# Reordering the stages of a two-layer graph and expert kernel: pairs' transposes, first residual, router and preparation

## The chip, the cores and the metric
The kernel runs on one core of a Trainium2 chip. Its engines are PE (TensorE: matrix products and transposes, PEld being its weight loads), DVE (VectorE), ACT (ScalarE) and POOL (GpSimd); SP issues most of the DMAs. Each engine takes its instructions strictly in the order in which the program lists them for it, and waits on semaphores for the others. The metric is the device time of one execution, in microseconds. Before the change it is 1788.81, the median of six runs (1777.96 to 1794.82).

## The reference
64 batches of 256 rows with 256 columns go through two layers. Each layer is a graph attention with a residual, then a feed-forward part with a residual; every part starts with a layer norm.

```
x = x + elu(gat0(norm(x), adj))          # 4 heads of 64, one shared 256 x 256 mask
x = x + norm(x) @ Wf.T + bf
x = x + relu(gat1(norm(x), adj))         # 1 head of 256
t = norm(x)
x = x + t + sum over e of combine[e] * (gelu(t @ w1[e]) @ w2[e])   # best 2 of 8 experts
```
The attention of a layer is softmax over neighbours of leaky_relu(e_src + e_dst), times the projected rows. All arithmetic is fp32. The expert part includes its own tokens, so its result is the normed rows plus the weighted expert outputs.

## The kernel before
**Stages of a batch.** A batch is 256 rows, held as two tiles of 128 partitions. `batch_layers` (from line 384) is a generator; each `yield` ends a segment. The outer loop (from line 913) counts steps and runs one segment of every active generator in each step. A new batch starts every third step, so 6 batches are under way at a time and one *period* of three steps issues one whole batch's worth of work. The number that a `yield` gives is the rank of the generator's next segment: within a step the segments run in rising rank, and among equal ranks the one that started first. So the program's order, which is each engine's order, is written out by the ranks. The segments, with the phase of the step (its number modulo 3) and the rank:

| segment | phase, rank | work |
|---|---|---|
| 0 | 0, 40 | load of the batch three ahead, norm of x (DVE), transposes `pt` (PE), copy to `xT` (ACT) |
| 1 | 1, 20 | first projection `pq` (L329, 268 columns), exponentials (L337 ACT), scaling of q (L341 DVE) |
| 2, 3 | 2, 10 and 0, 10 | scores of heads 0-1, then 2-3: `pd` (L353 PE), `z` (L360 DVE, four each) |
| 4 | 1, 50 | values `pv` (L374, 65 columns), `rinv` (L381 DVE), `hp` (L402 DVE) |
| 5 | 2, 20 | elu and residual: exponential (L408 ACT), x1 and x1b (L411, L412, L414 DVE) |
| 6 | 0, 30 | norm and transposes of x1 |
| 7 | 1, 70 | feed-forward `pf` (L422), x2 (L428 DVE), its norm |
| 8 | 2, 60 | transposes of x2 |
| 9 | 0, 20 | second projection `pq` (259 columns), exponentials, scaling |
| 10 | 1, 10 | second scores: two `pd`, two `z` |
| 11 | 2, 40 | second values `pv` (257 columns), `rinv` |
| 12 | 0, 5 | relu (L445 ACT) |
| 13 | 1, 60 | x2 plus relu, norm |
| 14, 15 | 2, 15 and 0, 50 | bias and scale; normed rows `xe` and `base` (L463, L468 ACT) |
| 16 | 1, 35 | `base` to the output (SP), transposes of `xe` |
| 17 | 2, 50 | router product `pl` (L489), logits `lg` (L493); with a chunk's last batch also `top_two` (L509) |

The reciprocal square roots of the norms are taken on POOL (L308, L309), for two batches at once.

**Routing and experts.** Batches are grouped into chunks: twelve of 4, six of 2, two of 1; two more batches are computed densely. After a chunk's last router product, `route` ranks the rows, sends each row to the regions of its two experts in DRAM (POOL, L755), and queues `expert_pair` jobs of 256 rows. A pair starts in phase 2. Its segments: load of its rows `xr` (rank 90), load of the expert's weights `we` (phase 0, 90), transposes `px` with the copy `sT` on ACT and the columns `to` and `w` on DVE (phase 1, 40), hidden product `ph` and gelu (phase 2, 30), second product `py` and bias to `y` (phase 0, 80), scaling of y on ACT (phase 1, 2). A scatter-add (POOL, L695) adds the rows to the output, each waiting for earlier ones. One to three pairs start in a period, eight in four periods in the middle of the run. Until the first chunk is routed there are none.

**Buffers.** All products go to eight PSUM banks, named `bank`, handed out as they come free. `hp` has two buffers.

**Preparation.** Ahead of the loop the masks are transposed, each attention's weights get the columns that give e_src and e_dst and are centred (`gnn_weights`, L139: DVE products and sums, `center` on PE and DVE), then the feed-forward and the router weights are transposed. This part has no written order: the compiler sorts it, together with the first steps of the loop, by what is ready. The load of batch 0 is the first on SP's queue. Experts' weights are loaded and packed by eight generators, one started in each step from step 4 (`SETUP_AT`).

Of the kernel before, what the change touches and what calls it, by code (L numbers as in the profile page):

```python
# [26 lines left out]
def kernel(  # L27
# [17 lines left out]
    nc = tc.nc  # L45
    B, N, D = x.shape
    E = router.shape[0]
    H = 4
# [44 lines left out]
    def load_batch(b):  # L93
        t = io.tile([P, NT, D], F32, tag="xin", name=f"xin_{b}", bufs=6)
        nc.sync.dma_start(
            out=t, in_=x_rows[b * N : (b + 1) * N, :].rearrange("(t p) d -> p t d", p=P)
        )
        return t

    AHEAD = 3  # L100
    xin = {0: load_batch(0)}


    ident = const.tile([P, P], F32, tag="ident", name="ident")
# [8 lines left out]
    adj_i = work.tile([P, NT, N], adj.dtype, tag="z", name="adj_i", bufs=6)  # L113
    nc.scalar.dma_start(out=adj_i, in_=adj.rearrange("(t p) j -> p t j", p=P))

    masks = []
    for layer, op in enumerate((ALU.is_gt, ALU.not_equal)):
        mf = work.tile([P, NT, N], F32, tag="xT", name=f"maskf{layer}", bufs=4)
        nc.vector.tensor_scalar(mf, adj_i, 0.0, None, op0=op)
        pm = bank("pm", [NT, N])  # L120
        for t in range(NT):
            for j in range(NT):
                nc.tensor.transpose(
                    pm[:, j, t * P : (t + 1) * P], mf[:, t, j * P : (j + 1) * P], ident
                )
        m = const.tile([P, NT, N], F32, tag=f"mask{layer}", name=f"mask{layer}")
        nc.vector.tensor_copy(m, pm)
        masks.append(m)

    def center(w, cols):  # L130

# [7 lines left out]
    def gnn_weights(w, a, heads, slope, name):  # L139

        d = D // heads
        wx = const.tile([P, KT, heads, d + 3], F32, tag=name, name=name)
        for k in range(KT):
            nc.sync.dma_start(
                out=wx[:, k, :, :d],  # L150
                in_=w[k * P : (k + 1) * P, :].rearrange("p (h d) -> p h d", h=heads),
            )
        av = work.tile([P, 2, d], F32, tag="e", name=name + "_a", bufs=1)
        nc.scalar.dma_start(out=av.rearrange("p s d -> p (s d)"), in_=rows_to_all(a, 2 * d))
        prod = work.tile([P, heads, d], F32, tag="hp", name=name + "_p")
# [14 lines left out]
        flat = wx.rearrange("p k h c -> p k (h c)")  # L170
        center(flat, heads * (d + 3))
        return flat

    wx0 = gnn_weights(w0, a0, H, SLOPE0, "wx0")
    wx1 = gnn_weights(w1g, a1g, 1, SLOPE1, "wx1")
# [5 lines left out]
    pw = bank("pw", [KT, D])  # L181
    for t in range(KT):
        for k in range(KT):
            nc.tensor.transpose(
                pw[:, k, t * P : (t + 1) * P], wf_in[:, t, k * P : (k + 1) * P], ident
            )
    nc.vector.tensor_copy(wfT, pw)
    center(wfT, D)
# [3 lines left out]
    nc.vector.tensor_scalar(bias_f, bias_f, -1.0, None, op0=ALU.add)  # L192
# [4 lines left out]
    pr = bank("pr", [KT, E])  # L197
    for k in range(KT):
        nc.tensor.transpose(pr[:, k, :], r_in[:, k * P : (k + 1) * P], ident[:E, :E])
    nc.vector.tensor_copy(rT, pr)  # L200

# [41 lines left out]
    def fill_spare():  # L243
# [7 lines left out]
        based.append(d.ins)  # L251
        yield 90


    setup = [lambda e=e: pack_expert(e) for e in range(E)] + [fill_spare]


    tri = const.tile([P, P], F32, tag="tri", name="tri")
# [125 lines left out]
    def batch_layers(b, c0, xng, lg):  # L384
# [12 lines left out]
        scores(q, H, range(2, 4), masks[0], probs)  # L397
        yield 50
        pvs, rinv = attended(q, H, probs)
        hp = work.tile([P, NT, D], F32, tag="hp", name="hp")  # L400
        for t, pv in enumerate(pvs):
            nc.vector.tensor_tensor(  # L402
                hp[:, t, :].rearrange("p (h d) -> p h d", h=H), pv[:, :, :HD],
                rinv[:, t, :, None].to_broadcast([P, H, HD]), ALU.mult,
            )
        yield 20
        ex = work.tile([P, NT, D], F32, tag="e", name="e", bufs=1)
        nc.scalar.activation(ex, hp, AF.Exp)  # L408

# [24 lines left out]
        xT = transposed(x2)  # L434
        yield 20
        q = projected(xT, wx1, 1, rstd)
        yield 10
        probs = []
        scores(q, 1, range(1), masks[1], probs)
        yield 40  # L440
# [41 lines left out]
            based.append(d.ins)  # L482
            nc.sync.nop()
        xT = transposed(xe[:, :, :D], *(("xTd", DENSE) if dense else ()))
        yield 50
        pl = bank("pl", [NT, E])
        for t in range(NT):
            for k in range(KT):
# [109 lines left out]
    def expert_pair(j, n, ids, ef, regs, needs):  # L598

        i = j % GROUP  # L600
        upto = min(j + GROUP, n)
        if i == 0:
            _, regs["e"] = nc.values_load_multi_w_load_instructions(
                ids[0:1, 0, j:upto], engines=[mybir.EngineType.SP], min_val=0, max_val=E - 1,
                skip_runtime_bounds_check_because=WHY,
            )
            _, regs["t"] = nc.values_load_multi_w_load_instructions(
                ids[0:1, 1, j:upto], engines=[mybir.EngineType.SP], min_val=0, max_val=E * CAP,
                skip_runtime_bounds_check_because=WHY,
            )  # L610
# [12 lines left out]
        we = io.tile([P, WROW], F32, tag="we", name="we", bufs=WBUFS)  # L623
        nc.sync.dma_start(
            out=we, in_=wpack[bass.ds(e_sp, 1), :, :].rearrange("e p c -> (e p) c")
        )
        yield 40
        px = bank("px", [KT, PAIR])
        for t in range(2):
            for k in range(KT):  # L630
                nc.tensor.transpose(  # L631
                    px[:, k, t * P : (t + 1) * P], xr[:, t, k * P : (k + 1) * P], ident
                )
# [132 lines left out]
    def later(rank):  # L766

        yield rank
        while (len(order_steps) - 1) % TICKS == 0:
            yield rank  # L770

    def route(c, row0, nt, n, last, xng, lg):
# [135 lines left out]

    batches = jobs()
    step, more, credit = 0, True, 0.0  # L910
    SETUP_AT = 4
    with tc.manual_schedule():
        while more or active or waiting or dense_jobs or scatters:
            phase = step % TICKS
# [63 lines left out]
```

## Time and profile before
| | us |
|---|---|
| median of six runs | 1788.81 |
| profiled execution, its own time | 1774.68 |
| its span, first to last instruction | 1773.0 |
| PE busy | 1578.4 |
| DVE busy | 1294.2 |
| ACT busy | 834.8 |
| POOL busy | 839.4 |

Busy time counts instructions that run on the engine. An idle time in brackets stands before the instruction that ended it, with what released it: `[0.64 <-ACT xT L319]` says that the engine stood for 0.64 us until ScalarE's copy to xT had ended. A PE group `x8` has eight matmul records, since a product in fp32 leaves two; a transpose leaves one. The mean granted PE clock is 0.962 of full speed. Times are from the span's start. The page's own limits hold: ends of matmuls are modelled, and a wait for several things is put down to the last.

The run falls into a head (to about 25 us, up to the first projection), a filling without expert pairs (to about 278, where the first pair is transposed), a middle, and a tail after the last batch (from about 1450), where pairs and dense experts remain.

### The profile page before, as it was taken

To read this page: it belongs to the slowest core of one execution; us is meant where nothing else is said; L and a number is where in the kernel's file an instruction comes from. 1 tells how busy PE (TensorE), PEld (TensorE's weight loads), DVE (VectorE), ACT (ScalarE), POOL (GpSimd) and SP (SyncE) were. 2 spreads that over 40 slices of the span, in tenths; PEclk is the share of its full clock that TensorE was granted. 3 is DMA by queue.
4 is the path that set the end of the run, shared out by engine and by line. 5 is a ranking of instruction groups with operands and counts; after the bars stand their busy time and mean duration, and the time that the engine had idled before them with its cause. 6 is when DMAs were issued, how large, how long until landed. Compare 5 with 4: busy or idle time off the path is not lost. (4 is left out here: it accounts for less than half of the span.)

```text
span 1773.0 us, 29975 instructions
## 1 busy us (share of the span) xinstructions
PE 1578.4 (89%) x9254; PEld 1389.3 (78%) x9254; DVE 1294.2 (73%) x4808; ACT 834.8 (47%) x1773; POOL 839.4 (47%) x788
## 2 busy tenths in 40 slices
PE   5898889799999999999999999999989998698791
PEld 4787777688888888888888888888878887577681
DVE  6888888978787878878787878789788886522231
ACT  1233324355555555555554555555455554533340
POOL 1111333426455564646464646565564655634444
PEclk9999999999999999999999999999999999888896
DMA  3510112135445453545453445445354455674753
GB/s 105 168 37 24 61 42 71 54 106 114 130 110 136 105 135 81 125 109 129 113 126 89 100 123 114 130 111 136 83 132 110 113 118 136 166 189 96 172 109 42
DMA packets 137372, 192.89 MB, mean 109 GB/s; under 512 B 18680, under 2 KB 91392, under 8 KB 137216
## 3 DMA queue, kind: packets, MB, share of 16 engines
q1 hardware_dynamic: 86592, 122.61, 22.4%
q0 software_dynamic: 49632, 67.39, 20.9%
q8 instruction: 76, 1.25, 0.3%
q10 hardware_dynamic: 992, 0.99, 0.2%
q14 instruction: 80, 0.66, 0.1%
HBM read 101.77 MB, written 89.15 MB: 108 GB/s over the span
## 5 line engine op out<-in xcount | busy, mean ns | idle before, releaser
L695 POOL DMA_INDIRECT out_dram<-y,to x262 | 419.4, 1601 | 302.0 <-DMA out_dram<-y,to 133.1
L374 PE MATMUL pv<-q,z 128*128 128x65 f32 (+1 forms) x2560 | 363.9, 297 | 8.0 <-DVE y L684 7.4
L374 PEld LDWEIGHTS pv<-q,z 128*128 128x128 f32 x2560 | 335.2, 194 | 23.2 <-DVE y L684 9.1
L329 PE MATMUL pq<-wx,xT 128*128 128x268 f32 (+1 forms) x1024 | 269.2, 407 | 39.8 <-ACT xT L319 33.6
L308 POOL TENSOR_SCALAR rstd<-mv 128x4 f32<-128x4 f32 (+1 forms) x132 | 39.3, 298 | 544.3 <-DVE mv L301 481.7
L663 PE MATMUL ph<-sT,we 128*128 128x256 f32 x1048 | 251.0, 396 | 43.5 <-ACT sT L635 21.6
L755 POOL DMA_INDIRECT xs<-xng,pos x248 | 251.2, 1013 | 69.1 <-issue 68.3
L360 DVE SCALAR_TENSOR_TENSOR z<-pd,q,mask 128x256 f32<-128x256 f32 x640 | 265.0, 472 | 7.1 <-PE pd L353 7.0
L678 PE MATMUL py<-w2s,hT 128*128 (+1 forms) x1176 | 264.1, 379 | 0.6 <-ACT hT L669 0.6
L663 PEld LDWEIGHTS ph<-sT,we 128*128 128x128 f32 x1048 | 204.2, 200 | 73.5 <-ACT sT L635 22.8
L329 PEld LDWEIGHTS pq<-wx,xT 128*128 128x128 f32 x1024 | 190.5, 196 | 89.9 <-ACT xT L319 54.1
L678 PEld LDWEIGHTS py<-w2s,hT 128*128 128x128 f32 x1176 | 219.4, 190 | 28.8 <-ACT hT L669 1.0
L319 ACT COPY xT<-pt 128x512 f32<-128x512 f32 x256 | 144.6, 588 | 203.8 <-PE pt L315 149.3
L684 DVE TENSOR_TENSOR y<-py,b2s 128x512 f32<-128x512 f32 x147 | 96.5, 687 | 146.5 <-PE py L678 70.8
L669 ACT ACTIVATE hT<-ph,we 128x256 f32<-128x256 f32 x294 | 123.2, 470 | 160.7 <-PE ph L663 120.2
L656 ACT ACTIVATE y<-y,w 128x256 f32<-128x256 f32 x262 | 112.8, 497 | 172.0 <-DVE y L684 162.6
L341 DVE SCALAR_TENSOR_TENSOR q<-pq,rstd,q 128x256 f32<-128x256 f32 x256 | 112.0, 478 | 91.0 <-ACT q L337 90.8
L300 DVE BATCH_NORM_STATS2 stats<-x 128x6 f32<-128x256 f32 x384 | 156.4, 407 | 2.2
L309 POOL TENSOR_TENSOR rstd<-rstd,mhalf 128x4 f32<-128x4 f32 (+1 forms) x132 | 135.9, 1029 | 10.9
L422 PE MATMUL pf<-wfT,xT 128*128 128x256 f32 x512 | 128.5, 395 | 0.0
L353 PE MATMUL pd<-ident,q 128*128 128x128 f32 x640 | 104.1, 278 | 11.8 <-ACT q L337 8.8
L408 ACT ACTIVATE e<-hp 128x512 f32<-128x512 f32 x64 | 40.3, 630 | 153.3 <-DVE hp L402 150.4
(147 smaller groups left out, 2106.7 us busy)
## 6 DMA issues: line engine op xcount, KB each, us to landing
we<-wpack SPq DMA_DIRECT2D x147, 288.0 KB
xr<-xs SPq DMA_DIRECT2D x131, 260.0 KB
xin<-in_x_dram SPq DMA_DIRECT2D x64, 256.0 KB
out_dram<-base SPq DMA_DIRECT2D x64, 256.0 KB
out_dram<-y,to POOLq DMA_INDIRECT x262
xs<-xng,pos POOLq DMA_INDIRECT x248
xs<-fill SPq DMA_DIRECT2D x9, 260.0 KB
wpack<-wt SPq DMA_DIRECT2D x8, 288.0 KB
```

The costliest lines, as they stand in the source:

```text
L300: nc.vector.bn_stats(stats[:, t, :], src[:, t, :])
L309: nc.gpsimd.tensor_tensor(rstd[:, :n], rstd[:, :n], mhalf[:, :n], ALU.pow)
L319: nc.scalar.copy(dst, pt)
L329: nc.tensor.matmul(pq.rearrange("p h c -> p (h c)"), xT[:, k, t * P : (t + 1) * P], wx[:, k, :], start=(k == 0), stop=(k == KT - 1),)
L360: nc.vector.scalar_tensor_tensor(z[:, j, :], pd[:, i, :], q[:, j, h, d + 2 : d + 3], mask[:, j, :], op0=ALU.max, op1=ALU.mult,)
L374: nc.tensor.matmul(pv[:, h, :], z[:, j, t * P : (t + 1) * P], q[:, j, h, : d + 1], start=(j == 0), stop=(j == NT - 1),)
L422: nc.tensor.matmul(pf[:, t, :], xT[:, k, t * P : (t + 1) * P], wfT[:, k, :], start=(k == 0), stop=(k == KT - 1),)
L663: nc.tensor.matmul(ph[:, f, :], we[:, k * D + f * P : k * D + (f + 1) * P], xT[:, k, :], start=(k == 0), stop=(k == KT - 1),)
L669: nc.scalar.activation(hT[:, f, :], ph[:, f, :], AF.Gelu, bias=we[:, C_B1 + f : C_B1 + f + 1])
L678: nc.tensor.matmul(py[:, t, :], hT[:, f, t * P : (t + 1) * P], w2s[:, e, f * D : (f + 1) * D].rearrange("p e c -> p (e c)"), start=(f == 0 ...
L695: d = nc.gpsimd.indirect_dma_start(out=out_rows, out_offset=bass.IndirectOffsetOnAxis(ap=to[:, t : t + 1], axis=0), in_=y[:, t, :], in_off ...
L755: d = nc.gpsimd.indirect_dma_start(out=xs_d[: E * CAP * PAIR, :], out_offset=bass.IndirectOffsetOnAxis(ap=at, axis=0), in_=xe, in_offset=None,
```

## The change
Ranks: `px` of a pair goes from 40 to 60 in phase 1, so behind `pv` (50) and segment 13 (60, started earlier) and ahead of `pf` (70). Segment 5 goes from 20 to 5, ahead of the scores in phase 2. Segment 10 goes from 10 to 25, behind the first projection in phase 1. Segment 17 goes from 50 to 35 in phase 2, ahead of the second values (40).

Preparation: the first attention's weight loads are issued ahead of the load of batch 0. The second attention's columns (`prepare1`), the feed-forward weights (`prepare_f`), the second mask and the router's transposes become generators that run at rank 90 in steps 1 to 4, in the order feed-forward, second attention, mask, router; their loads stay ahead of the loop. The experts' packing follows from step 5. `hp` and the preparation's `prod`, which share a tag, get one buffer. The test in `later` is written with the last step number instead of the count of steps.

```diff
-    xin = {0: load_batch(0)}
...
+    def fill_mask(layer, op):
...
+    fill_mask(0, ALU.is_gt)
...
+        return flat, lambda: score_columns(wx, av, heads, slope, name)
...
+    wx0, prepare0 = gnn_weights(w0, a0, H, SLOPE0, "wx0")
+    xin = {0: load_batch(0)}
+    prepare0()
+    wx1, prepare1 = gnn_weights(w1g, a1g, 1, SLOPE1, "wx1")
...
+    def once(work):
+        work()
+        return
+        yield
...
+    setup = [
+        lambda work=work: once(work)
+        for work in (prepare_f, prepare1, lambda: fill_mask(1, ALU.not_equal), prepare_r)
+    ]
+    setup += [lambda e=e: pack_expert(e) for e in range(E)] + [fill_spare]
...
-        hp = work.tile([P, NT, D], F32, tag="hp", name="hp")
+        hp = work.tile([P, NT, D], F32, tag="hp", name="hp", bufs=1)
...
-        yield 20
+        yield 5
         ex = work.tile([P, NT, D], F32, tag="e", name="e", bufs=1)
...
         q = projected(xT, wx1, 1, rstd)
-        yield 10
+        yield 25
         probs = []
...
-        yield 50
+        yield 35
         pl = bank("pl", [NT, E])
...
-        yield 40
+        yield 60
         px = bank("px", [KT, PAIR])
...
-        while (len(order_steps) - 1) % TICKS == 0:
+        while order_steps[-1] % TICKS == 0:
...
-    SETUP_AT = 4
+    SETUP_AT = 1
```

More of the change, by code (lines that the diff above doesn't have):

```diff
@@ L114 @@
     nc.scalar.dma_start(out=adj_i, in_=adj.rearrange("(t p) j -> p t j", p=P))
-    masks = []
-    for layer, op in enumerate((ALU.is_gt, ALU.not_equal)):
+    masks = [
+        const.tile([P, NT, N], F32, tag=f"mask{layer}", name=f"mask{layer}") for layer in range(2)
+    ]
+    def fill_mask(layer, op):
         mf = work.tile([P, NT, N], F32, tag="xT", name=f"maskf{layer}", bufs=4)
@@ L125 @@
                 )
-        m = const.tile([P, NT, N], F32, tag=f"mask{layer}", name=f"mask{layer}")
-        nc.vector.tensor_copy(m, pm)
-        masks.append(m)
+        nc.vector.tensor_copy(masks[layer], pm)
+    fill_mask(0, ALU.is_gt)
     def center(w, cols):
@@ L154, in gnn_weights, with score_columns @@
         nc.scalar.dma_start(out=av.rearrange("p s d -> p (s d)"), in_=rows_to_all(a, 2 * d))
-        prod = work.tile([P, heads, d], F32, tag="hp", name=name + "_p")
+        flat = wx.rearrange("p k h c -> p k (h c)")
+        return flat, lambda: score_columns(wx, av, heads, slope, name)
+    def score_columns(wx, av, heads, slope, name):
+        d = D // heads
+        flat = wx.rearrange("p k h c -> p k (h c)")
+        prod = work.tile([P, heads, d], F32, tag="hp", name=name + "_p", bufs=1)
         for k in range(KT):
@@ L169, in gnn_weights @@
             )
-        flat = wx.rearrange("p k h c -> p k (h c)")
         center(flat, heads * (d + 3))
-        return flat
-    wx0 = gnn_weights(w0, a0, H, SLOPE0, "wx0")
-    wx1 = gnn_weights(w1g, a1g, 1, SLOPE1, "wx1")
+    wx0, prepare0 = gnn_weights(w0, a0, H, SLOPE0, "wx0")
+    xin = {0: load_batch(0)}
+    prepare0()
+    wx1, prepare1 = gnn_weights(w1g, a1g, 1, SLOPE1, "wx1")
     wf_in = work.tile([P, KT, D], F32, tag="xT", name="wf_in", bufs=4)
@@ L180, with prepare_f @@
     wfT = const.tile([P, KT, D], F32, tag="wfT", name="wfT")
[L181 to L188, printed above, removed]
     bias_f = const.tile([P, D], F32, tag="bias_f", name="bias_f")
     nc.scalar.dma_start(out=bias_f, in_=rows_to_all(bf, D))
-    nc.vector.tensor_scalar(bias_f, bias_f, -1.0, None, op0=ALU.add)
+    def prepare_f():
+        pw = bank("pw", [KT, D])
+        for t in range(KT):
+            for k in range(KT):
+                nc.tensor.transpose(
+                    pw[:, k, t * P : (t + 1) * P], wf_in[:, t, k * P : (k + 1) * P], ident
+                )
+        nc.vector.tensor_copy(wfT, pw)
+        center(wfT, D)
+        nc.vector.tensor_scalar(bias_f, bias_f, -1.0, None, op0=ALU.add)
     r_in = work.tile([E, D], F32, tag="x1b", name="r_in")
@@ L196, with prepare_r @@
     rT = const.tile([P, KT, E], F32, tag="rT", name="rT")
[L197 to L200, printed above, removed]
+    def prepare_r():
+        pr = bank("pr", [KT, E])
+        for k in range(KT):
+            nc.tensor.transpose(pr[:, k, :], r_in[:, k * P : (k + 1) * P], ident[:E, :E])
+        nc.vector.tensor_copy(rT, pr)
     C_B1, WROW = KT * D, KT * D + 64
@@ L252, in fill_spare @@
         yield 90
-    setup = [lambda e=e: pack_expert(e) for e in range(E)] + [fill_spare]
+    def once(work):
[5 more added lines that the diff above has]
+        for work in (prepare_f, prepare1, lambda: fill_mask(1, ALU.not_equal), prepare_r)
+    ]
+    setup += [lambda e=e: pack_expert(e) for e in range(E)] + [fill_spare]
     tri = const.tile([P, P], F32, tag="tri", name="tri")
```

## The prediction
> **What bounds the kernel now.** I read the page's busy shares first, then busy time by stage, then the table of who waits for whom, and last the order of time inside one period of each stage. The shares of the page:
> ```profile
> PE 1578.4 (89%) x9254; PEld 1389.3 (78%) x9254; DVE 1294.2 (73%) x4808; ACT 834.8 (47%) x1773; POOL 839.4 (47%) x788
> ```
> By stage (columns: busy us and count of PE, PEld, DVE, ACT, POOL, then clock, DMA share, GB/s): the head, the filling before the expert pairs come, and the steady middle.
> ```profile
> 0.00:25.30 25.30, 10.86 (x31) 6.83 (x31) 13.45 (x49) 1.87 (x2) 3.19 (x16) 1.00 0.41 122
> 90.00:354.40 264.40, 228.77 (x1405) 196.93 (x1403) 229.71 (x813) 91.08 (x220) 75.27 (x94) 0.96 0.16 48
> 354.40:1210.00 855.60, 821.63 (x5004) 733.51 (x5005) 683.68 (x2459) 472.77 (x980) 462.70 (x428) 0.99 0.46 114
> ```
> The middle is PE's (96% busy). The filling is as much VectorE's: 229.71 us against PE's 228.77. The waits that the reordering touches (total us, times, longest):
> ```profile
> DVE q L341 <- ACT q L337: 90.8, 83, 3.4
> DVE rinv L381 <- PE pv L374: 80.0, 69, 3.2
> PE pq L329 <- ACT xT L319: 33.6, 84, 0.7
> PE px L631 <- DMA xr<-xs: 16.7, 15, 2.0
> PE pv L374 <- DVE y L684: 7.4, 10, 1.6
> ```
> VectorE waits most for the small exponentials that its own scaling of q needs; PE's removable waits are the pairs' rows (16.7) and a PSUM bank (7.4). One period of the filling, in order of time:
> ```profile
> 105.34 0.23 DVE L381 RECIPROCAL rinv<-pv 128x1 f32<-128x1 f32 x2
> 105.54 0.84 ACT L445 ACTIVATE rel<-pv,rinv 128x256 f32<-128x256 f32 x2 [2.60 <-DVE rinv L381]
> 106.56 1.09 ACT L319 COPY xT<-pt 128x512 f32<-128x512 f32 x2
> 107.70 2.07 PE L329 MATMUL pq<-wx,xT 128*128 128x268 f32 x8 [0.64 <-ACT xT L319]
> 110.04 0.84 DVE L360 SCALAR_TENSOR_TENSOR z<-pd,q,mask 128x256 f32<-128x256 f32 x2
> 111.96 0.88 DVE L341 SCALAR_TENSOR_TENSOR q<-pq,rstd,q 128x256 f32<-128x256 f32 x2 [1.07 <-ACT q L337]
> 113.77 0.18 DVE L381 RECIPROCAL rinv<-pv 128x4 f32<-128x4 f32 x1 [0.85 <-PE pv L374]
> ```
> This is a closed loop of 16.7 us with nothing loose in it: VectorE to the second layer's reciprocal, ScalarE's relu, exponential and two copies, PE's first projection and values, VectorE again. The z of 110.04 (second layer's scores) runs while the q of 111.96 is still waiting: it costs nothing there. The same stretch of a middle period after routing, when VectorE is behind:
> ```profile
> 907.22 2.00 PE L374 MATMUL pv<-q,z 128*128 128x65 f32 x16 [0.59 <-DVE y L684]
> 907.68 0.86 DVE L360 SCALAR_TENSOR_TENSOR z<-pd,q,mask 128x256 f32<-128x256 f32 x2
> 909.10 0.88 DVE L341 SCALAR_TENSOR_TENSOR q<-pq,rstd,q 128x256 f32<-128x256 f32 x2 [0.55 <-ACT q L337]
> 918.70 0.23 DVE L381 RECIPROCAL rinv<-pv 128x1 f32<-128x1 f32 x2
> 919.75 1.28 ACT L337 ACT_TABLE_LOAD   x1
> 922.48 2.07 PE L329 MATMUL pq<-wx,xT 128*128 128x268 f32 x8 [0.64 <-ACT xT L319]
> 927.29 0.63 PE L631 MATMUL px<-ident,xr 128*128 128x128 f32 x4 [1.36 <-DMA xr<-xs]
> ```
> VectorE is busy from 909.10 to 920.56 without a gap; its reciprocal at 918.70 sets relu, table load, exponential, copies and so PE's projection at 922.48. Then PE is the late one again and waits 1.36 for the third pair's rows.
>
> **The change, part by part.** *Late preparation.* The first projection starts here:
> ```profile
> 25.28 2.07 PE L329 MATMUL pq<-wx,xT 128*128 128x268 f32 x8 [0.68 <-ACT xT L319]
> ```
> Its weights wait in VectorE's queue behind the other layer's preparation, which stood 2.77 for its vector (to 14.38). With that moved, wx0's columns end near 11.0 as now, the centring's matmuls (1.26) near 12.4, its two subtractions (0.77) near 13.2; with hand-overs the projection starts at 13.5, 11.8 sooner. Against it, VectorE's 8.0 moves into steps 1 to 4, where one batch is in flight and every engine is on its path: prepare1 4 x 0.42 + 4 x 0.41 + 4 x 0.15 + 0.77 = 4.7, prepare_f 0.69 + 0.75 + 0.29 = 1.7, the second mask 0.76 + 0.68 = 1.4, the router's copy 0.2. PE's transposes and centrings there (1.06 + 2.08 + 1.07 + about 1.0 + 0.38 = 5.6) lie beside VectorE's but for hand-overs, which I put at 1.3. Sum -2.5; the ends are -11.8 (all hidden) and +1.3 + 8.0 - 11.8 + 5.6 = +3.1 (PE's hidden nowhere). On SP's queue the first x load moves behind two weight loads (four of these took 3.70 to issue, so 1.85 later; rows landed by 5.63, needed at 12): nothing. The experts' loads, five each on SP, start one step later; the first pair is transposed at 278.6: nothing. ScalarE's queue still holds its copies behind the second vector's load, which waits for the first one's use (10.38 now); its table load of 1.28 is over by 12: nothing.
>
> *Second-layer scores behind the projection (10 to 25).* On VectorE z now stands behind q. Where q waits, the wait grows by the 0.84 to 0.87 that z covered, and z itself comes after. On PE two pd transposes (107 ns apart each, 0.22) no longer fill a wait in front of the projection.
> *Pairs' transposes behind the first values (40 to 60).* PE: pv, and with it rinv and hp, come 0.44 sooner for each pair; the third pair's wait of 1.36 is covered by the values' 3.5. ScalarE's sT copies (0.59 each) still end before ph, since pf (1.95) and pd (0.60) lie between. VectorE: `to` and the two `w` (0.43 a pair) pass from before rinv, where it waits anyway, to behind the next batch norm; together with the earlier pv about +0.1 for two pairs. The bank that pv takes changes too, so its wait on y goes.
> *First residual ahead of scores (20 to 5).* Same VectorE work, x1 1.65 sooner and the first z 2.1 later; that z is read a step and a half later by pv, so nothing. Its bank comes free 2.1 later. Where VectorE lags, it ends at 916.44 and the x transposes that could take the bank start at 918.77, so I take 0. The ends are -0.3 a period (half of the filling's pt waits on x1, 9.0 in 15 periods) and, should the second projection of 916.92 get that bank, 2.1 - 0.5 = +1.6 in one period of four.
> *Router ahead of the second values (50 to 35).* PE does the same in another order. VectorE copies the logits (0.15) before rinv, and in one period of four the top-two choice (12 operations, 3.0) as well. In the middle that period has ScalarE's copies waiting till 877.4 although the exponential was done at 875.6, so the later relu fits; price 0 there. In the filling it delays the loop.
> *`later`* tests the same step number as before, and hp with one buffer is written a full period after it was read: nothing.
>
> **The sum**, against the profiled execution (span 1773.0, its own time 1774.68, that is 14.1 below the median 1788.81 of the runs). Filling: 8 tight loops each get 0.15 + 0.22 = 0.37, so +3.0; three routing passes, two periods each, where VectorE never catches up, get 0.85 for the uncovered q in both, and 0.35 for the top-two choice ahead of the reciprocal, so 3 x 2.05 = +6.2. Ends: -4.5 (only the pt half) and +13 (0.87 in all 15). Middle, 9 chunks of four batches: VectorE's chain to the projection +0.87 + 0.15 + 0.1, pd +0.22, the pairs' rows -1.36: 0.0 each. The 0.59 for y and 0.29 for the second projection are swallowed, as the projection waits for the chain anyway. Ends 9 x (-2.0) = -18 (chain not longer) and 9 x (1.34 + 1.6) = +26 (rows still waited for, the bank too). Last stretch, 8 routings in the periods from 1190 on: 8 x 1.34 = 10.7, less the rows' waits there (0.5 + 1.9 + 1.1 + 1.7 + 1.8 = 7.0): +3.7. After that no order changes that matters. Sum -2.5 + 3.0 + 6.2 + 0.0 + 3.7 = +10.4: 1785.1 for the profiled execution, 1799 for the median.
>
> A page of the Trainium skill may be set beside this. The row first: the stretch behind PE's longest filling wait (3.41, ended at 176.13) ran at half clock.
> ```profile
> 178.10:184.90 6.80, 6.32 (x21) 5.03 (x20) 6.29 (x37) 2.88 (x6) 0.00 (x0) 0.50 0.27 80
> ```
> The waits of 0.64 in the list above were not followed by one in every period. "TensorE: Matmul & The Clock Gate", section "Why this matters for your kernels", says that a pause of about 3 us between bursts sets the clock back to half. The projection's wait would grow from 0.64 to some 2.0, so by the rule nothing is added.
> By the rows it is open, as 2.0 lies between 0.64 and 3.41. Such a stretch of 6.8 at half speed costs 3.4; one in each of the 9 chunks would put 9 x 3.4 = +31 on top. I take none.
>
> **The rivals.** *The chain does not lengthen* (the other side). Place: the q of 909.10. If ScalarE's exponential is ready when y ends, z behind q costs nothing, the filling keeps its loop, and the waits for rows and y go: -16.7 - 7.4 = -24.1, 1765. For it: ScalarE is 47% busy. Against it: the exponential there stands behind the scaling of y (1.70), which follows VectorE's y. It decides below 0.4 us of extra wait a period. *Hidden anyway*: preparation keeps 7 more of its 11.8, which cancels most of the filling's loss: about 1790. For it: VectorE idles 11.8 of the first 25.3. *The clock*: PE's gathered wait brings half-speed stretches, about 1825 with most of the 31. Against it: middle waits of 1.3 to 2.0 before the pairs exist now, and four stretches only between 600 and 1300.
>
> **How the numbers follow.** Forecast 0.40, at 1799, its own range 1785 to 1812; the chain rival 0.22, hidden 0.24, the clock 0.14. Within 0.5% (1780 to 1798, about what a measurement of this kernel can tell) fall most of the hidden case (0.20) and 0.12 of the forecast; faster get the chain rival's 0.22 and 0.01; slower the rest. The range runs from 1766, the chain rival's time, to 1824, short of the clock's.
>
> **What would show it.** Right: px without a DMA wait worth naming; first projection near 13 to 15; q's wait on ScalarE's exponential up from 90.8 towards 130; the projection's waits on xT longer but fewer in the middle; pd and pv waits gone; a filling period of 17.1. Wrong: a period of 16.7 or less, q's wait unchanged, the fourth batch's projection (57.70 now) 8 or more sooner, or half-clock stretches in every chunk.

## The result and the profile after

The changed kernel takes 1792.16 us (median of 34 runs, 1784.36 to 1798.65) where the kernel before takes 1782.65 (76 runs, 1768.29 to 1800.82) beside it: 1.006 times, 95% interval 1.0046 to 1.0074. It is slower, and the forecast of +10.4 had the sign and nearly the size. But the experiments show that the sum came out right because several of its terms were wrong in opposite directions.

The profiled execution of after has a span of 1786.0 (its own time 1787.69), 13.0 more than before. Its busy shares, from the page:
```profile
PE 1576.5 (88%) x9254; PEld 1389.4 (78%) x9254; DVE 1290.5 (72%) x4808; ACT 837.5 (47%) x1773; POOL 874.3 (49%) x788
```
PE, VectorE and ScalarE have the same work as before within 4 us (POOL's busy time, which is rough, reads 874.3 for 839.4); the time is in waits and in the clock. By stage (columns as before): the head, the filling, the middle, cut at the first projections of the same batches as the rows shown of before.
```profile
0.00:15.10 15.10, 4.51 (x13) 2.65 (x13) 6.71 (x28) 1.87 (x2) 3.13 (x16) 1.00 0.66 205
95.70:373.00 277.30, 229.90 (x1405) 199.23 (x1405) 229.91 (x815) 92.25 (x221) 82.33 (x93) 0.94 0.15 46
373.00:1219.90 846.90, 812.73 (x5005) 726.71 (x5005) 682.40 (x2462) 474.63 (x980) 485.54 (x429) 1.00 0.47 116
```
The filling now takes 277.30 (264.40 before, with the same 1405 matmul records), the middle 846.90 (855.60 before, PE's clock 1.00 where it was 0.99). The clock of 1.00 in the row of the head is no reading: this trace's clock records begin at 19.5. The table of waits of after:
```profile
ACT rel L466 <- DVE rinv L402: 144.1, 48, 6.5
DVE q L362 <- ACT q L358: 122.3, 75, 3.3
ACT sT L656 <- PE px L652: 84.8, 40, 3.6
PE pq L350 <- ACT xT L340: 67.0, 78, 4.9
DVE rinv L402 <- PE pv L395: 51.2, 59, 1.6
PEld pt L336 <- DVE z L381: 20.4, 16, 1.8
```
VectorE's wait for q's exponential rose from 90.8 to 122.3 and PE's for xT doubled from 33.6; ScalarE's relu waits 144.1 for the second layer's reciprocal (89.0 before). The waits of px for rows fall from 16.7 to 5.8, all of it in the tail, and those of pv for y (7.4 before) are gone. The last line is new: PE's transposes of the next batch wait for the first scores' z, whose PSUM bank they take.

One period of the filling with a routing in it, in order of time. First before, where the top-two choice (lines `top` to `oh`) stands behind the reciprocal:
```profile
155.46 0.23 DVE L381 RECIPROCAL rinv<-pv 128x1 f32<-128x1 f32 x2
155.66 0.84 ACT L445 ACTIVATE rel<-pv,rinv 128x256 f32<-128x256 f32 x2 [2.60 <-DVE rinv L381]
155.79 0.22 DVE L517 TENSOR_REDUCE top<-lg 128x8 f32<-128x64 f32 x1
158.36 0.23 DVE L525 TENSOR_TENSOR oh<-em,least 128x64 f32<-128x64 f32 x1
```
Then after:
```profile
146.52 2.07 PE L350 MATMUL pq<-wx,xT 128*128 128x268 f32 x8 [1.77 <-ACT xT L340]
150.69 0.88 DVE L362 SCALAR_TENSOR_TENSOR q<-pq,rstd,q 128x256 f32<-128x256 f32 x2 [1.84 <-ACT q L358]
151.48 0.87 DVE L381 SCALAR_TENSOR_TENSOR z<-pd,q,mask 128x256 f32<-128x256 f32 x2
161.20 0.22 DVE L538 TENSOR_REDUCE top<-lg 128x8 f32<-128x64 f32 x1
163.78 0.23 DVE L546 TENSOR_TENSOR oh<-em,least 128x64 f32<-128x64 f32 x1
164.18 0.23 DVE L402 RECIPROCAL rinv<-pv 128x1 f32<-128x1 f32 x2
164.37 0.84 ACT L466 ACTIVATE rel<-pv,rinv 128x256 f32<-128x256 f32 x2 [5.64 <-DVE rinv L402]
```
The wait of q is 1.84 where it was 1.07, and z stands uncovered behind it, as the prediction had it. The top-two choice now runs from 161.20 to 164.18 in front of the reciprocal, and ScalarE stands for 5.64 instead of 2.60. The projection behind this, and its two sisters at the next routings, from PE's own instructions:
```profile
166.53 3.60 PE L350 MATMUL pq<-wx,xT 128*128 128x268 f32 x8 [4.86 <-ACT xT L340]
245.72 3.94 PE L350 MATMUL pq<-wx,xT 128*128 128x268 f32 x8 [4.86 <-ACT xT L340]
329.87 3.75 PE L350 MATMUL pq<-wx,xT 128*128 128x268 f32 x8 [4.86 <-issue]
1326.63 3.76 PE L350 MATMUL pq<-wx,xT 128*128 128x268 f32 x8 [4.24 <-ACT xT L340]
```
A wait of 4.86 instead of 1.77 is 3.1 more each time, and the eight matmuls after it take 3.60 to 3.94 instead of 2.07: half clock. The last line is one of two such waits in the last stretch (the other, 4.17, ended at 1219.85). The head of after:
```profile
15.05 3.94 PE L350 MATMUL pq<-wx,xT 128*128 128x268 f32 x8 [0.68 <-ACT xT L340]
24.13 0.41 DVE L166 TENSOR_TENSOR wx_p<-wx,wx_a 128x256 f32<-128x256 f32 x1
28.04 1.23 PE L137 MATMUL pc<-wx,mean_w 128*128 128x259 f32 x2 [0.74 <-DVE wx L174]
29.06 1.06 PE L374 MATMUL pd<-ident,q 128*128 128x128 f32 x4
31.01 0.59 ACT L340 COPY xT<-pt 128x512 f32<-128x512 f32 x1 [11.71 <-PE pt L336]
33.36 1.09 PE L125 MATMUL pm<-ident,maskf 128*128 128x128 f32 x4 [2.38 <-DVE maskf L121]
34.24 3.12 PE L350 MATMUL pq<-wx,xT 128*128 128x268 f32 x8
```
Batch 0's projection starts 10.23 sooner (15.05 for 25.28), though its eight matmuls take 3.94 for 2.07, but batch 1's comes at 34.24 where it came at 29.81: the centring `pc` of the second layer stands in PE's queue behind four microseconds of VectorE's products, and the second half of batch 0's `pd`, whose q had been ready since 19.83, and the transposes of batch 1 stand behind `pc`; the mask's `pm` then holds up the projection in the same way.

The middle's lag period (the one behind a routing, in which VectorE is late), to be set beside 907.22 to 927.29 of before:
```profile
921.60 0.88 DVE L362 SCALAR_TENSOR_TENSOR q<-pq,rstd,q 128x256 f32<-128x256 f32 x2 [1.52 <-ACT q L358]
922.39 0.87 DVE L381 SCALAR_TENSOR_TENSOR z<-pd,q,mask 128x256 f32<-128x256 f32 x2
932.00 0.22 DVE L402 RECIPROCAL rinv<-pv 128x1 f32<-128x1 f32 x2
935.77 2.07 PE L350 MATMUL pq<-wx,xT 128*128 128x268 f32 x8 [1.47 <-ACT xT L340]
941.86 1.48 PE L652 MATMUL px<-ident,xr 128*128 128x128 f32 x12
```
q waits 1.52 (0.55 before), z comes after it, the projection waits 1.47 (0.64 before), and the three pairs' transposes run without a wait.

### The profile page after: what moved, and what is told of

Its sections match the earlier page's. It is cut to its first block, busy times and chain, and to the rows that moved or that the text cites. A ratio compares the mean times of both kernels' runs of the same rounds, so it can differ in the third digit from the quotient of the medians.

```text
span 1786.0 us, 29982 instructions
## 1 busy us (share of the span) xinstructions
PE 1576.5 (88%) x9254; PEld 1389.4 (78%) x9254; DVE 1290.5 (72%) x4808; ACT 837.5 (47%) x1773; POOL 874.3 (49%) x788
## 5 line engine op out<-in xcount | busy, mean ns | idle before, releaser
L350 PE MATMUL pq<-wx,xT 128*128 128x268 f32 (+1 forms) x1024 | 278.4, 418 | 81.2 <-ACT xT L340 67.0
L395 PEld LDWEIGHTS pv<-q,z 128*128 128x128 f32 x2560 | 329.9, 193 | 13.9 <-issue 2.5
L329 POOL TENSOR_SCALAR rstd<-mv 128x4 f32<-128x4 f32 (+1 forms) x132 | 56.4, 427 | 513.6 <-DVE mv L322 445.8
L350 PEld LDWEIGHTS pq<-wx,xT 128*128 128x128 f32 x1024 | 198.1, 202 | 139.0 <-ACT xT L340 88.1
L699 PEld LDWEIGHTS py<-w2s,hT 128*128 128x128 f32 x1176 | 219.5, 190 | 28.8 <-ACT hT L690 1.0
L362 DVE SCALAR_TENSOR_TENSOR q<-pq,rstd,q 128x256 f32<-128x256 f32 x256 | 112.0, 479 | 146.1 <-ACT q L358 122.3
L705 DVE TENSOR_TENSOR y<-py,b2s 128x512 f32<-128x512 f32 x147 | 97.4, 688 | 144.3 <-PE py L699 81.5
L330 POOL TENSOR_TENSOR rstd<-rstd,mhalf 128x4 f32<-128x4 f32 (+1 forms) x132 | 157.9, 1196 | 10.9
L466 ACT ACTIVATE rel<-pv,rinv 128x256 f32<-128x256 f32 x128 | 53.9, 472 | 154.6 <-DVE rinv L402 144.1
L443 PE MATMUL pf<-wfT,xT 128*128 128x256 f32 x512 | 123.3, 384 | 0.4 <-DVE q L362 0.4
L656 ACT COPY sT<-px 128x512 f32<-128x512 f32 x131 | 69.9, 590 | 84.8 <-PE px L652 84.8
```

The lines of the kernel that those rows point to most:

```text
L330: nc.gpsimd.tensor_tensor(rstd[:, :n], rstd[:, :n], mhalf[:, :n], ALU.pow)
L350: nc.tensor.matmul(pq.rearrange("p h c -> p (h c)"), xT[:, k, t * P : (t + 1) * P], wx[:, k, :], start=(k == 0), stop=(k == KT - 1),)
L395: nc.tensor.matmul(pv[:, h, :], z[:, j, t * P : (t + 1) * P], q[:, j, h, : d + 1], start=(j == 0), stop=(j == NT - 1),)
L443: nc.tensor.matmul(pf[:, t, :], xT[:, k, t * P : (t + 1) * P], wfT[:, k, :], start=(k == 0), stop=(k == KT - 1),)
L699: nc.tensor.matmul(py[:, t, :], hT[:, f, t * P : (t + 1) * P], w2s[:, e, f * D : (f + 1) * D].rearrange("p e c -> p (e c)"), start=(f == 0 ...
```

## The experiments

Each stage's length below is the time between first projections, read from PE's instructions in each profiled execution (batches counted from 0). The stretch 8 to 20 lies in the filling, 20 to 54 is called the middle and 54 to 63 the last stretch. "Half" is the time at half clock and "idle" PE's and PEld's common idle time, both from batch 20 to 54.

| kernel | to batch 8 | 8 to 20 | 20 to 54 | 54 to 63 | 63 to end | end | half | idle |
|---|---|---|---|---|---|---|---|---|
| before | 141.1 | 242.1 | 805.6 | 224.7 | 359.5 | 1773.0 | 10.2 | 30.8 |
| after | 146.5 | 253.1 | 795.9 | 230.8 | 359.7 | 1786.0 | 0 | 28.4 |
| late_only | 146.5 | 242.5 | 813.7 | 224.9 | 357.9 | 1785.5 | 30.7 | 28.9 |
| ranks_only | 140.6 | 253.1 | 796.8 | 232.5 | 362.6 | 1785.6 | 0 | 28.7 |
| router_only | 145.4 | 257.7 | 818.1 | 227.0 | 358.4 | 1806.5 | 30.7 | 31.3 |
| scores_only | 145.6 | 248.7 | 810.6 | 228.1 | 362.0 | 1795.1 | 17.1 | 31.4 |
| pairs_only | 141.3 | 244.9 | 786.9 | 212.5 | 365.0 | 1750.6 | 0 | 18.8 |
| residual_only | 141.7 | 253.3 | 819.2 | 226.2 | 363.4 | 1803.8 | 34.1 | 31.0 |
| pairs_late | 147.7 | 239.1 | 787.3 | 212.6 | 364.5 | 1751.2 | 0 | 19.0 |
| after_again | 149.8 | 253.6 | 795.9 | 228.7 | 365.4 | 1793.4 | 0 | 28.4 |
| after_no_router | 146.8 | 249.0 | 795.4 | 219.5 | 365.7 | 1776.4 | 0 | 28.7 |
| after_no_scores | 147.5 | 253.2 | 788.6 | 225.6 | 361.4 | 1776.4 | 0 | 18.5 |
| after_no_residual | 148.1 | 258.4 | 796.9 | 228.8 | 361.6 | 1793.8 | 0 | 29.3 |
| pairs_sooner | 144.3 | 242.3 | 800.1 | 219.9 | 361.7 | 1768.2 | 6.8 | 26.5 |

The kernel before was not equally fast beside all of them: its median was 1794.08 beside the first four experiments, 1771.4 beside the next four, 1771.59 beside the last four. So times are compared with the runs of before that stand beside them, and across experiments only among the last eight. Each row of the table is one execution: the two of the changed kernel differ by 3.3 in the head, 2.1 in the last stretch and 5.7 in the tail, and before's lies 14.1 below the median of its six runs, that of scores_only 9.1 below.

**late_only: the preparation alone.**
```diff
-    setup = [lambda e=e: pack_expert(e) for e in range(E)] + [fill_spare]
+    setup = [
+        lambda work=work: once(work)
+        for work in (prepare_f, prepare1, lambda: fill_mask(1, ALU.not_equal), prepare_r)
+    ]
+    setup += [lambda e=e: pack_expert(e) for e in range(E)] + [fill_spare]
...
-    SETUP_AT = 4
+    SETUP_AT = 1
```
The rest of the edit is that of the change, with the one buffer of `hp` and the test in `later`, which no run takes apart.


> The kernel before with the late preparation alone (all ranks as before). Theory (the trace of after): the written order puts the preparation's matmuls in front of the batches' own on TensorE, each behind its VectorE chain; the first projection comes 10 us sooner (15), but batches 1 to 8 come about 5 us later, and nothing changes from there, so +5 at the end: 1.003. Rival (the prediction as made): the preparation gains 2.5, and what the changed kernel shows in its first 100 us comes from the ranks: 0.9986. Second rival: the head's loss is caught up where TensorE is not the bound and the end stays: 1.000.


Measured: 0.998 (0.9945 to 1.0014), 1791.26 against 1794.08: nothing that this comparison can tell. The head shows the theory's price: 146.5 to batch 8, where before takes 141.1. Over all profiled executions the seven kernels with the old head take 140.6 to 145.6 (mean 142.9) and the seven with the late preparation 146.5 to 149.8 (mean 147.6), so +4.7; from the first projection to batch 8, 20.5 to 27.3 us run at half clock with the late preparation and 0 to 13.7 without. The rival's -2.5 falls for the head; the time doesn't decide. The theory's "nothing changes from there" can't be read off this trace: its middle is 8.1 longer, with 20.5 more at half clock.

**ranks_only: the four ranks with the old preparation.** The edits are the four `yield` lines of the change.


> The four ranks of the change, with the preparation and its order as before. Theory: the head keeps its times (first projection 25.3, batch 8 within 1.5 of before), the filling loses about 11 by batch 20, the middle gains about 10, the last stretch loses about 6.5: +8 at the end, 1.0045. Rival (the prediction as made, whose ranks alone came to +12.9): 1.007, with nothing gained in the middle.


Measured: 0.9979 (0.9952 to 1.0006), 1791.83 against 1794.08. The stages are the theory's: head as before, filling +11.0, middle -8.8, last stretch +7.8, 12.7 at the end of the trace. The expected ratio missed, since before was itself slow there. Its time is that of the changed kernel (1791 to 1792): beside the ranks, the late preparation's longer head doesn't show in the total, though the two were not run side by side.

**router_only.**
```diff
-        yield 50
+        yield 35
         pl = bank("pl", [NT, E])
```


> The router's rank alone (50 to 35). Theory: in the filling the three routings put the twelve operations of the top-two choice (3.0 us) ahead of the second layer's reciprocal, and the projection behind it comes 3.3 later each time: +10 by batch 20; in the middle nothing, in the last stretch (8 routings) part of it: +10 to +16 at the end, 1.006 to 1.009. Rival (the prediction as made): 0.35 for each routing in the filling and 0.15 a period, nothing in the middle: +2 to +3, 1.0015.


Measured: 1.006 (1.0027 to 1.0093). The filling grows by 15.6, more than the theory's 10. Of this 9.3 fall on the three routing passes (batches 8 to 10, 12 to 14, 16 to 18), whose first period takes 19.9 for 16.7, and 6.3 on the three periods between and behind them (batches 11, 15, 19); 6.2 more are idle and twice the time runs at half clock (41.0 for 20.5 from batch 8 to 20). The projection itself waits 0.64 here; the wait stands ahead of it, at the scores' transposes (3.83 in the first pass). The rival's 2 to 3 is out.

**scores_only.**
```diff
         q = projected(xT, wx1, 1, rstd)
-        yield 10
+        yield 25
```


> The second layer's scores alone behind the first projection (10 to 25). Theory: the wait of q on the exponential rises from 91 us to some 120, a tight loop of the filling takes 0.2 more (TensorE's two transposes), a routing pass of it no more than 1, and the middle is unchanged: +2 to +5, 1.001 to 1.003. Rival (the prediction as made): 0.22 a tight loop and 0.85 in both periods of each routing pass, and 1.09 a chunk in the middle that only the moved pairs' transposes would give back: +5 in the filling, +10 in the middle, +8 in the last stretch, 1.013.


Measured: 1.0035 (0.9993 to 1.0077). q's wait is 135.6 (90.8 before), the projection waits 1.79 in the tight loops (0.64 before), and the filling takes 6.6 more: 0.2 in a tight loop (one without routing) and 1.8 to 1.9 in each routing pass, as the rival (my prediction) had it. The middle takes 5.0 more, of which half clock is (17.1 - 10.2) / 2 = 3.4; so the rival's +10 there isn't seen while the pairs' transposes stand at 40. The measured ratio covers the theory's and not the rival's 1.013. Each theory is half right.

**pairs_only.**
```diff
-        yield 40
+        yield 60
         px = bank("px", [KT, PAIR])
```


> The pairs' transposes alone behind the first values (40 to 60). Theory: TensorE's waits for the pairs' rows (about 1.4 a chunk) and for the bank that y held (0.6 a chunk) go, and with the rows' waits the half-clock stretches of the middle, which every version with the transposes at 40 shows and neither version with them at 60; nothing else changes: head and filling as before, -10 to -18 over the middle, -3 to -7 in the last stretch, -13 to -20 at the end, 0.989 to 0.993. Rival (the prediction as made, chain rival's price for this edit: the waits alone, -16.7 - 7.4 at most, but the chain of VectorE takes part over): -12, 0.993, and half-clock stretches as before. Second rival: the wait for the first projection takes the place of the rows' wait, 1.000.


Measured: 0.9888 (0.9846 to 0.9931), 1750.63 us: the theory's number at its far end, and this one line is faster than both kernels. The trace of pairs_only, filling and middle by stage and the lag period by time:
```profile
89.50:356.60 267.10, 231.76 (x1404) 198.48 (x1404) 230.34 (x815) 91.86 (x221) 75.22 (x94) 0.94 0.16 48
356.60:1193.60 837.00, 816.08 (x5005) 728.24 (x5005) 682.63 (x2458) 473.19 (x980) 462.01 (x428) 1.00 0.47 117
```
```profile
915.79 2.07 PE L329 MATMUL pq<-wx,xT 128*128 128x268 f32 x8 [0.64 <-ACT xT L319]
921.66 1.48 PE L631 MATMUL px<-ident,xr 128*128 128x128 f32 x12
```
The middle takes 837.00 for 855.60, and no wait takes the place of the rows': the projection still waits 0.64. From batch 20 to 54, 18.7 are gained; PE's idle time falls by 12.0, and the 10.2 at half clock, worth 5.1, are gone.

**residual_only.**
```diff
-        yield 20
+        yield 5
         ex = work.tile([P, NT, D], F32, tag="e", name="e", bufs=1)
```


> The first residual alone ahead of the scores (20 to 5). Theory (the trace of after): the bank of the first scores comes free later, and the transposes of the next batch wait 0.85 for it once a chunk: +7 over the middle; in the filling 0.3 a period less for the transposes of x1, at most -4 by batch 20; +2 to +5 at the end, 1.002. Rival (the prediction as made): 0 in the middle, -0.3 a period in the filling: 0.999.


Measured: 1.0149 (1.0097 to 1.0202). Both theories miss by far. The loss lies between batch 8 and 54, 24.8 longer; PE's idle time hardly changes there (+1.3), but 75.1 us run at half clock (30.7 before), worth 22.2. The routing passes are 0.7 shorter in all, 12.0 are lost in the periods of the filling between and behind them and 13.6 in the middle. One such stretch, in PE's instructions and then by stage:
```profile
950.61 1.09 PE L631 MATMUL px<-ident,xr 128*128 128x128 f32 x4 [2.11 <-DMA xr<-xs]
951.49 6.93 PE L374 MATMUL pv<-q,z 128*128 128x65 f32 x32
```
```profile
943.00:949.90 6.90, 5.05 (x29) 3.85 (x27) 4.69 (x15) 4.60 (x12) 5.12 (x5) 1.00 0.79 218
949.90:960.10 10.20, 9.49 (x41) 9.16 (x42) 3.08 (x16) 2.12 (x5) 3.19 (x2) 0.51 0.64 144
```
The values take 6.93 where they take 3.68 at full speed. Why the rows come later against PE in this version was not traced.

**pairs_late: the pairs' move with the late preparation.** The edits are those of pairs_only and late_only together.


> The pairs' transposes behind the first values, with the late preparation; the three other ranks as before. If the parts add up: the head of the late preparation (first projection near 15, batch 8 near +5 against the profiled execution of before, +1 against the other executions seen with that head), the filling as before, and the middle and last stretch of the pairs' move: -8 to -15 at the end against before, 0.991 to 0.996, and 12 to 20 below the changed kernel. Rival: in the filling and the middle the late preparation changes which banks are handed out, and the gain of the pairs' move is smaller with it: less than half of it.


Measured: 0.9913 (0.988 to 0.9946), 1754.82 us. The pairs' gain is whole with it (middle 787.3, last stretch 212.6, as alone). The medians differ by 4.2 from pairs_only, which fits the head's 4.7.

**after_again: the changed kernel once more**, without an edit.


> The changed kernel itself, on the same chip as the three others and timed against the same runs of before: 1.003 to 1.007, its middle without half-clock stretches. If the kernel before varies by chip, as its spread of 35 us in the last runs would have it, the ratio comes nearer to 1.000 while the changed kernel's own time stays near 1792.


Measured: 1790.95 us, as first measured, and 1.0105 (1.0061 to 1.0149) because before was at 1771.4 there. The head of this execution is 149.8 long (146.5 in the first trace) and the middle 795.9, as there. The wait of q comes to 148.2 in it, so that this sum is no fine measure.

**after_no_router.**
```diff
-        yield 35
+        yield 50
         pl = bank("pl", [NT, E])
```


> The changed kernel with the router's rank put back (35 to 50). Measured so far between the kernel with the pairs' move and late preparation alone and the changed kernel: the three other ranks cost 14 in the filling, 9 in the middle, 18 in the last stretch, 35 at the end (profiled executions). Theory: the router's part is the top-two choice ahead of the reciprocal, which the filling and the last stretch feel: about 7 of the 14 and 4 to 8 of the 18 go, the projection's waits of 4.9 in three routing passes of the filling go, nothing in the middle; 10 to 16 below the changed kernel. Rival (the prediction as made): 0.35 for each of three routings and 0.15 a chunk in the middle: 2 to 3 below.


Measured: 1774.2 us, 16.8 below after_again; 1.0019 (0.9994 to 1.0043) against before. The theory's range is just passed. Against after, the filling is 4.1 shorter (7.6 in the three routing passes, less 3.5 in the periods between and behind them, with 34.1 at half clock for 30.7), the middle the same, the last stretch 11.3 shorter: there the projection's waits of 4.2 shrink to the 1.39 and 1.11 of this version, and 6.8 run at half clock for 13.7.
```profile
1212.85 2.07 PE L350 MATMUL pq<-wx,xT 128*128 128x268 f32 x8 [1.39 <-ACT xT L340]
1313.56 2.07 PE L350 MATMUL pq<-wx,xT 128*128 128x268 f32 x8 [1.11 <-ACT xT L340]
```

**after_no_scores.**
```diff
-        yield 25
+        yield 10
         probs = []
```


> The changed kernel with the second layer's scores put back ahead of the first projection (25 to 10). Theory: VectorE's wait of q on the exponential goes back from 122 us to about 90; the filling gets 3 to 6, the middle about 1 a chunk (VectorE's chain of the lag period is 0.87 shorter and TensorE has its two transposes back in front of the projection), the last stretch 6 to 10: 16 to 24 below the changed kernel. Rival: the router and the residual cost the 35, and the scores, whose z merely changes its place in VectorE's queue, give less than 8 back.


Measured: 1775.76 us, 15.2 below after_again; 1.002 (0.9994 to 1.0046). q's wait falls to 101.3 and the projection's to 37.4. The middle gets 7.3 (idle 28.4 to 18.5), the last stretch 5.2, the filling as a whole nothing (253.2). Yet its loop is shorter: a tight loop takes 16.7 for 16.9, and the three routing passes together 2.9 less. The periods between and behind them take 3.0 more, beside half-clock stretches that the trace of after does not have in the same places (34.1 us at half clock for 30.7). The other execution of the changed kernel has one at the first of these places too, so this part is not shown to belong to the edit.

**after_no_residual.**
```diff
-        yield 5
+        yield 20
         ex = work.tile([P, NT, D], F32, tag="e", name="e", bufs=1)
```


> The changed kernel with the first residual put back behind the scores (5 to 20). Theory: the transposes of the next batch no longer wait for the bank of the scores (16.6 us in 16 waits, 0.85 a chunk in the middle), and the transposes of x1 wait for x1 again in the filling: -7 in the middle, +2 to +5 in the filling, 2 to 6 below the changed kernel. Rival (the prediction as made): 0 in the middle, 0.3 a period more in the filling: 4 above.


Measured: 1795.4 us, 4.4 above after_again; 1.0142 (1.0114 to 1.0171). The time is the rival's, the mechanism only in part: the filling is 5.3 longer, but a tight loop only 0.1 where the rival has 0.3 a period, the routing passes 2.3 together, and the half-clock time grows by 10.2, worth 5.1. The middle is 1.0 longer. The wait for the bank of z is nearly gone (1.3), but the transposes of x1 wait 22.3 for x1 instead, so the bank wait brought no loss on balance.

**pairs_sooner: the transposes the other way.**
```diff
-        yield 40
+        yield 30
         px = bank("px", [KT, PAIR])
```


> The kernel before with the pairs' transposes the other way, ahead of the router's (40 to 30): their wait for the rows is doubled, nothing else moves but four transposes of 0.60 in all. Theory (TensorE's wait for rows brings the half-clock stretches): a wait of 1.4 a chunk becomes about 2.0, of the length after which the single changes showed stretches of 6.8 to 10.2; most of the twelve chunks get one, and the time rises by 20 to 45, 1.012 to 1.025. Rival (the stretches come by chance and not from these waits): two or three stretches in the middle as before, +5 to +8 at the end, 1.004.


Measured: 1.0026 (0.9998 to 1.0053). The theory's number is out, but so is its dose: the waits for rows in eight chunks fell to 7.4 in all where before has 11.0. The run doesn't decide between the two; it only shows that four transposes earlier do not double the wait.

## Why the prediction was right, and where it was not

The sum was +10.4 and the measured difference 9.5 in the first comparison (1792.16 - 1782.65) and 19.6 in the second (1790.95 - 1771.4). By stage the prediction had -2.5 for the head, +9.2 for the filling, 0.0 for the middle and +3.7 for the last stretch; the profiled execution has +5.4, +11.0, -9.7 and +6.1. The head, the filling and the last stretch together cost 12.1 more than forecast and the middle 9.7 less, so the errors nearly cancel. Term by term:

- **The scores behind the projection** were priced at 0.85 to 1.09 a period, which adds up to 6.9 in the filling, 9.8 in the middle and 8.7 in the last stretch. The mechanism is shown: q's wait rose to 122.3 (towards 130, as forecast), z is uncovered, and the projection's wait in the middle went from 0.64 to 1.47. Alone it took 6.6 in the filling, period by period as priced; taken out of the changed kernel it gave 2.9 in the routing passes, which longer periods elsewhere in the filling offset, 7.3 in the middle and 5.2 in the last stretch. In all 15.2 where I had 25: in the filling the terms of the scores and of the top-two choice overlap, and in the other two stages a quarter to two fifths of the terms was too much.
- **The router** is the step that failed: "0.35 for the top-two choice ahead of the reciprocal" in each filling pass, and 0.15 a period besides. The prediction gives the choice 3.0 and no working for the 0.35. But relu, exponential, copy and projection hang on that reciprocal, so all of the choice's 3.0 lands on the loop: alone it makes the first period of a pass 19.9 for 16.7, and with the scores moved too the projection waits 4.86 for 1.77, three times, with a stretch at half clock at each. Per pass that comes to 2.6 to 3.8 alone and to 2.0 to 3.3 in the changed kernel. The last stretch has two such waits as well, and the router's part there came to 11.3, where I had 1.2. In all 16.8 where my terms add up to about 5. The middle's 0 was right (795.4 with and 795.9 without it undone).
- **The pairs' transposes**: I gave 1.36 a chunk, 12.2 over nine, and 7.0 in the last stretch, less 0.1 a period for VectorE, so 17.5; 20.8 in all was measured for the edit alone (1771.4 to 1750.63). The covered waits are shown. My middle of 0.0 was -9.7: the pairs' gain there is 18.3 (pairs_late against before), since pv's wait for y, which I had called swallowed, and the half-clock time go as well, and the chain's price of 8.6 (after against pairs_late) stands against the 1.34 a chunk that I set (11.4 for the 8.5 chunks of that stretch).
- **The late preparation**: -2.5 with an upper end of +3.1; the head is +4.7 by the means above, and the time +4.2 with the pairs' move alone. With all ranks moved it doesn't show (1791.83 without the late preparation, 1791 to 1792 with it), so its price in the changed kernel stays open between 0 and 5. The step that failed is that PE's transposes and centrings "lie beside VectorE's but for hand-overs, which I put at 1.3". They do not: written into the queue, they stand in front of the batches' matmuls and pass VectorE's delay on to them (`pd` with its q ready at 19.83, run at 29.06), and more of the head runs at half clock (20.5 us for 10.2 up to batch 8). The first projection's own gain (10.2 for 11.8) was right.
- **The residual** at 0: taken out of the changed kernel it costs 4.4, in size the end of -0.3 a period that I named and did not take; but where no pair is in flight a period gains only 0.1, and the rest stands beside half-clock time. The bank wait (16.6 us in 16 waits) came at the transposes for which I had taken 0, but it replaces waits for x1. Alone, with the pairs' transposes at 40, the same edit costs 28 (1799.75 against 1771.4), which nothing in the prediction has.
- **The tail** at 0: 359.5 and 359.7.
- **The rivals**: "the chain does not lengthen" fell with q's wait. "The clock" turned out the other way round in the middle: no half-clock stretch at all there, with waits of 1.47, while the versions with the transposes at 40 have them. "Hidden anyway" has no support, as the head got longer.
- **The signs**: a filling period takes 16.9, between the 17.1 of the forecast and the 16.7 that would have refuted it; the fourth batch's projection comes at 61.14 for 57.70.

So +16.8, +15.2, -4.4, +4.2 and -20.8 stand for +5, +25, 0, -2.5 and -17.5 of mine. The first three, taken back one at a time, add up to 27.6, while together they cost 36.1 (1790.95 against 1754.82); the rest belongs to their joint action and was not taken apart. A right total was largely luck: the router was 12 too cheap and the scores 10 too dear, and the head's loss and the middle's gain were both missed.

## What to carry to other kernels

When a step is moved ahead of another on an in-order engine, price all that it issues against the first instruction behind it that another engine waits for; a reciprocal of 0.2 us can carry a whole loop. Work with long hand-overs that a compiler had sorted by readiness lost in the head here when its order was written out by hand, since each matmul that waited held the ready ones behind it. And a bundle of five edits should be taken apart: here one line was worth -1.1% and the rest took it back and more.

## What was not expected of the hardware

In the six kernels that have the pairs' transposes ahead of the values, PE's waits from batch 20 to 54 can be set against the clock. Summed over each group of pairs, all seven waits for rows of 2.08 to 3.69 were followed by 6.8 to 10.2 us at half clock, and of the 39 of 1.99 or less only one (1.33). The Trainium skill, "TensorE: Matmul & The Clock Gate", section "Why this matters for your kernels", warns of gaps above some 3 us; here all five waits of 4.2 to 4.9 of the changed kernel came with half clock, but so did single waits of 2.1 to 2.4.

But these eight stretches are 75 us of the 130 that the six kernels spend at half clock there. The other 13 stretches, of 3.4 or 6.8 us, each began 0.8 to 2.0 us after the start of values that had waited only 0.56 to 0.66 for a bank of y. One of them, from late_only, where `pf` takes 3.72 for the 1.89 of full speed:
```profile
1010.77 2.87 PE L395 MATMUL pv<-q,z 128*128 128x65 f32 x16 [0.65 <-DVE y L705]
1013.44 3.72 PE L443 MATMUL pf<-wfT,xT 128*128 128x256 f32 x8
```
Of 48 such waits in the six kernels 35 were not followed by half clock, so the length of a wait does not decide alone. In the other eight kernels neither wait occurs in that stretch, the projection waits up to 1.6, and there was no stretch at half clock. This is a coincidence of waits and clock in traces; the one run meant to lengthen the waits for rows did not lengthen them, so that either wait is the cause is argued and not shown. The kernel before, which has such stretches, had medians from 1771 to 1794 between comparisons, while the changed kernel, which has none in its middle, stayed at 1791 to 1792 in two; whether the one explains the other was not tested.
